# Handing a chunk's scaled rows from row layout to channel layout: VectorE squares and a trip through DRAM in place of TensorE transposes

## The chip, the core and the metric

The kernel runs on one core of a Trainium2 chip, in 32-bit floating point throughout. The core has five instruction queues: TensorE (PE; its weight loads are listed apart as PEld), VectorE (DVE), ScalarE (ACT), GpSimd (POOL) and SyncE (SP, which here only issues DMAs). Each queue runs its instructions in the order in which they were written, and an instruction that waits holds up everything behind it on its own queue; between queues the order is kept by semaphores. The metric is the device time in microseconds (us); lower is better. The kernel before takes 794.65 us, the median of 6 runs (792.32 to 797.26).

## The reference

Four sequences of 1024 tokens with 256 channels each go through an attention-like block (a gated linear recurrence along the sequence) and then a mixture of 8 experts of which each token takes 2; both halves are modulated per sequence. Cut to what matters:

```python
mod = (silu(c) @ wmod).reshape(4, 6, 1, -1)
sa, ca, ga, sb, cb, gb = (mod[:, i] for i in range(6))
ga, gb = clamped away from zero
h = layernorm(x) * (1 + ca) + sa
x = x + ga * attn(h)
h = layernorm(x) * (1 + cb) + sb
x = x + gb * ffn(h)

def attn(x):                                  # per sequence, D = 256, H = 512
    norm = l2norm(x) * D ** -0.5
    xn = rms_scale * x / (norm + EPS) * split_scale
    K = sigmoid(xn @ W_K)
    u, g_in, g_out = split(xn @ W_ugg, 3)
    u = u * sigmoid(g_in) * (1 - K)
    out = linear_scan(shifted K, u)           # s[t] = K[t-1] * s[t-1] + u[t]
    return out * sigmoid(g_out) @ W_out + x

def ffn(x):                                   # 8 experts, 256 -> 1024 -> 256
    scores = softmax(x @ Wg + bg); take the best 2, renormalise
    return sum over the 2 experts of score * (gelu(x @ W1[e] + b1[e]) @ W2[e] + b2[e])
```

## The kernel before

The 4096 tokens go through the first half in 8 chunks of 512 tokens (`for c_ in range(NCH)`, L990; two chunks make a sequence, `part` is 0 or 1). A chunk lies in two layouts: by rows (tokens on the 128 partitions, 4 groups of 128 tokens, 256 channels along the free axis) for the norms and the modulation, and by channels (`hT`: channels on the partitions, 2 groups of 128, 512 tokens along the free axis) as the moving operand of the projections. `ident` is the identity matrix that a TensorE transpose uses.

`project(c_, hc)` (L396) is called four times per chunk, once for each 128 of the 512 hidden channels. It makes four products of two matmuls each, `pk`, `pgi`, `pu`, `pgo`, in four PSUM banks that rotate (pool `ps_mm`, 4 buffers): so a product of one call can only start when the product of the same name of the call before has been read out of its bank. ScalarE reads `pk` (L421), `pgi` (L425) and `pgo` (L429), VectorE reads `pu` (L428), and then VectorE makes the recurrence (L431, L437, L438) into `z`. The list `mid` holds steps that are written between the reading of `pgi` and that of `pu`.

The order of all five queues is written out by hand (`manual_schedule`, L101). While chunk c is projected, three other pieces of work are threaded into the gaps:

- the head of chunk c+1, called `nxt`: the layer norm on ScalarE (`shift`, `a_norm`), modulation on VectorE (`a_mod`, L355 and L356), the sum of squares on ScalarE into tile `u` (`a_square`, L365), the root on VectorE and GpSimd (`a_root`, L371 and L372), the inverse and the scaling on VectorE (`a_scale`, L376, L377, L379), and the turning (`a_turn`, L387): 8 TensorE transposes of 128x128 into PSUM (L393) and two ScalarE evictions that also multiply each channel by `rs_sb` (L394). All of this happens within chunk c: `a_norm` in `project(c, 0)`, `a_square` in `project(c, 1)`, `a_scale` before `project(c, 2)`, `a_turn` in `project(c, 3)`.
- the tail of chunk c-1, called `prv`: the output projection (`o_pe`, L448, products `pya`), the residual (`o_resid`, L461, and its store L464), the second layer norm (`f_stats`, `f_norm`, `f_mod`, `f_store`), and `f_swap` (L503) at the chunk's end. `f_swap` already turns rows to channels without TensorE: VectorE transposes each 32x32 square of the rows into `u` (L508), SyncE stores that to DRAM (`swapped`, L512) and, once it has landed, loads it back with the squares exchanged in four loads (L519). The result `hT2` is the operand of the routing matmuls (`f_gate`, `pl`, L558) a chunk later.
- the routing of finished sequences, in some chunks only: `r_softmax`, `r_exp`, `r_first` in chunks 3, 5 and 7; `r_second` (some 18 small VectorE operations, L621 to L660), `r_rank_pe` (three small TensorE products `pr`, L667 to L674, on what `r_second` made) and `r_place` in chunks 4 and 6. `r_place` leaves 16 indirect scatters to the DRAM table `lists` (L580), which GpSimd issues six at a time in `drain` (L576).

Tile `u` has one buffer (`bufs=1`), shared by `a_square`/`a_scale` of the head and by `f_swap` of the tail: whoever writes it next waits until the one before has been read, and for `f_swap` the last reader is the DMA of L512.

In the last chunk SyncE starts the experts' weight loads (L837, L839) and the loads of the table entries (L808), GpSimd gathers the first block's rows (L820), and TensorE turns them in `project(7, 3)` (`b_turn(0)`, products `ptx`, L878). From 299 us on the second half runs: blocks of 256 rows of one expert, `b_up` (`ph`, L898) and `b_down` (`pye`, L928).

Of the kernel before, what the change touches and what calls it, by code (L numbers as in the profile page):

```python
# [19 lines left out]
def tile_adaln_block(  # L20
# [32 lines left out]
    nc = tc.nc  # L53
# [319 lines left out]

    def a_scale(c_):
        h, ss, u = X[c_]["h"], X[c_]["ss"], X[c_]["u"]
        nc.vector.tensor_scalar_add(ss, ss, RMS_EPS)  # L376
        nc.vector.reciprocal(ss, ss)  # L377
        for n in range(TPB):
            nc.vector.tensor_scalar_mul(u[:, n, :], h[:, n, :], ss[:, n : n + 1])  # L379

# [5 lines left out]

    def a_turn(c_):  # L387
        hT = deep.tile([P, KC, TB], F32, tag="hT", name=f"hT_{c_}")
        X[c_]["hT"] = hT
        for k in range(KC):  # L390
            pt = ps_tr.tile([P, TB], F32, tag="tr", name=f"pta_{c_}_{k}")
            for t in range(TPB):
                nc.tensor.transpose(pt[:, ts(t, P)], X[c_]["u"][:, t, ts(k, P)], ident)  # L393
            nc.scalar.activation(hT[:, k, :], pt, AF.Copy, scale=rs_sb[:, k : k + 1])  # L394

    def project(c_, hc, mid=()):  # L396


        hT = X[c_]["hT"]
# [8 lines left out]
        def product(w, col, what):  # L408
            ps = ps_mm.tile([P, TB], F32, tag="mm", name=f"p{what}_{c_}_{hc}")
            for k in range(KC):  # L410
                nc.tensor.matmul(  # L411
                    ps,
                    lhsT=w[:, k, col : col + P],
                    rhs=hT[:, k, :],
                    start=(k == 0),
                    stop=(k == KC - 1),
                )
            return ps
# [79 lines left out]


    turned = [P, NQ, KC, TPB, SQ]  # L500
    swapped = dram.tile([NQ, NQ, SQ, KC * TB // NQ], F32, tag="swapped", name="swapped")

    def f_swap(c_):  # L503


        u = work.tile([P, TPB, D], F32, tag="u", name=f"u2_{c_}", bufs=1)
        flat = u.rearrange("p n d -> p (n d)")
        nc.vector.transpose(  # L508
            flat.rearrange("p (q k n c) -> p n k q c", q=NQ, k=KC, n=TPB),
            X[c_]["h2"].rearrange("p n (k q c) -> p n k q c", k=KC, q=NQ),  # L510
        )
        nc.sync.dma_start(  # L512
            out=swapped.rearrange("q i c m -> (i c) q m"),
            in_=flat.rearrange("p (q m) -> p q m", q=NQ),
        )
        hT = deep.tile(turned, F32, tag="hT2", name=f"hT2_{c_}", bufs=1)
        X[c_]["hT2"] = hT
        for q in range(NQ):
            nc.sync.dma_start(  # L519
                out=hT[ts(q, SQ)].rearrange("p i k n t -> p i (k n t)"),  # L520
                in_=swapped[q].rearrange("i c m -> c i m"),
            )
# [456 lines left out]
    hT = deep.tile([P, KC, TB], F32, tag="hT", name="hT_0")  # L979
    X[0]["hT"] = hT  # L980
# [4 lines left out]
    nc.scalar.activation(hT[:, 0, :], pts[0], AF.Copy, scale=rs_sb[:, 0:1])  # L985
    nc.vector.tensor_scalar_mul(hT[:, 1, :], pts[1], rs_sb[:, 1:2])
# [3 lines left out]
    for c_ in range(NCH):  # L990
# [10 lines left out]
        if more:  # L1001
            shift(nxt)
        project(c_, 0, [lambda: a_norm(nxt)] if more else [])
        drain(6)
        if more:
            a_mod(nxt)
        if was:
            a_skip(c_)
            o_pe(prv)
            o_resid(prv)  # L1010
        if placed is not None:
            r_second(placed)
# [8 lines left out]
        project(c_, 1, [lambda: a_square(nxt)] if more else [])  # L1021
# [27 lines left out]
        if more:  # L1049
            a_root(nxt)  # L1050
# [6 lines left out]
        if more:  # L1057
            a_scale(nxt)
# [18 lines left out]
        project(c_, 3, [lambda: a_turn(nxt) if more else b_turn(0)])  # L1077
# [125 lines left out]
```

## Time and profile before

| | us |
|---|---|
| median of 6 runs | 794.65 (792.32 to 797.26) |
| the profiled execution's own time | 795.89 |
| its span, first to last instruction | 794.1 |
| chunk 4 (from the end of its first projection call to that of chunk 5) | 36.58 |
| chunk 5, the same | 36.02 |
| chunk 6, the same | 36.59 |
| TensorE busy in the span | 774.6 |

The profile is of one execution. Its instruction tables give a line of the kernel, the engine, the operation, the tiles (what is written, an arrow, what is read), how often, and how long. A timeline row gives start, duration and, in square brackets, how long the engine stood idle before it and what ended that. Matmuls overlap their neighbours, so the time that one costs TensorE is read from the distance between two starts, not from its duration: the four records of a 128x512 product show 1.88 us but start 1.72 us apart from the next product. A matmul in 32-bit floating point leaves two records; a transpose leaves one. "SPq" and "POOLq" are the queues that issue DMAs; a DMA row there is only the issue, and the landing is told apart.

### The profile page before, as it was taken

What the parts mean: (1) busy time and instruction counts of PE and PEld (TensorE: products, weight loads), DVE (VectorE), ACT (ScalarE), POOL (GpSimd) and SP (SyncE); (2) the same over time, 40 slices, a digit from 0 to 9 for tenths busy, and PEclk for the clock granted to TensorE, in tenths of its full rate; (3) what the DMA queues carried; (4) which work ended last, traced back from release to release, by engine and by line L of the source; (5) the groups of instructions that cost most, each with busy time, mean ns of one, the idle gap of its engine ahead of it and who ended that gap; (6) DMA issues with size and microseconds to landing.
All of it is one profiled execution on the core that took longest, in us unless ns stands there. A gap on an engine that the chain in (4) does not pass through costs nothing.

```text
span 794.1 us, 10818 instructions
## 1 busy us (share of the span) xinstructions
PE 774.6 (98%) x3279; PEld 579.1 (73%) x3279; DVE 506.7 (64%) x1369; ACT 241.8 (30%) x560; POOL 295.6 (37%) x372
## 2 busy tenths in 40 slices
PE   8999999999999999999999999999999999999974
PEld 5454545464555647888888888888888888888964
DVE  5787877899789968777453535454453535445653
ACT  4434243535354242322131222222131222213221
POOL 2102010107302830888843434343343424344421
PEclk9999999999999999999999999999999999999997
DMA  8221434052322367799797878777786787776691
GB/s 293 92 71 47 129 104 126 27 172 57 79 80 87 79 195 236 177 228 221 182 291 217 228 220 213 202 220 235 212 236 209 222 222 211 213 209 198 190 297 32
DMA packets 115463, 138.11 MB, mean 174 GB/s; under 512 B 25207, under 2 KB 99515, under 8 KB 115393
## 3 DMA queue, kind: packets, MB, share of 16 engines
q1 hardware_dynamic: 96368, 111.45, 47.2%
q0 software_dynamic: 17456, 25.25, 14.2%
q8 instruction: 32, 0.52, 0.3%
q10 hardware_dynamic: 1568, 0.57, 0.3%
q14 instruction: 39, 0.31, 0.1%
HBM read 114.31 MB, written 25.42 MB: 176 GB/s over the span
## 4 chain that ended last, share of the span: by engine, by line
PE 84%; DMA 7%; issue 3%; DVE 3%; ACT 1%; POOL 1%; POOLq 0%; SPq 0%; DVEq 0%
PE pye_False L928 24%; PE ph_False L898 24%; PE pya L448 7%; PE pk L411 7%; PE pgi L411 7%; PE pu L411 6%; PE pgo L411 6%; DMA out_dram<-yb_False,ent 3%; DMA hb<-hx,ent 3%; PE idle L257 1%; PE pta L393 1%; DMA ent<-lists 1%; PE pm L284 1%; DMA w<-in_L_ffn_W_dram 1%; POOL out_dram L915 1%
## 5 line engine op out<-in xcount | busy, mean ns | idle before, releaser
L928 PE MATMUL pye_False<-w,g_False 128*128 128x256 f32 x992 | 219.5, 379 | 0.0
L898 PE MATMUL ph_False<-xT,w 128*128 128x256 f32 x992 | 219.3, 379 | 0.0
L898 PEld LDWEIGHTS ph_False<-xT,w 128*128 128x128 f32 x992 | 188.3, 190 | 26.3 <-issue 0.5
L928 PEld LDWEIGHTS pye_False<-w,g_False 128*128 128x128 f32 x992 | 188.2, 190 | 25.9 <-issue 0.2
L907 ACT ACTIVATE g_False<-ph_False,bb 128x256 f32<-128x256 f32 x248 | 103.8, 470 | 301.4 <-issue 197.5
L885 DVE STREAM_TRANSPOSE xT<-hb 32x128 f32<-32x128 f32 x576 | 174.2, 302 | 21.5 <-DMA hb<-hx,ent 8.3
L942 DVE TENSOR_TENSOR yb_False<-pye_False,b2b 128x256 f32<-128x256 f32 x62 | 26.3, 424 | 185.7 <-PE pye_False L928 185.7
L915 POOL DMA_INDIRECT out_dram<-yb_False,ent x46 | 73.8, 1604 | 178.6 <-DVE yb_False L943 178.6
L580 POOL DMA_INDIRECT lists<-pay,placei x64 | 66.5, 1040 | 12.5 <-issue 11.0
L820 POOL DMA_INDIRECT hb<-hx,ent x56 | 58.9, 1051 | 20.7 <-issue 16.9
L411 PE MATMUL pk<-hT,wk_sb 128*128 128x512 f32 x128 | 61.0, 599 | 0.7 <-ACT hT L985 0.7
L411 PE MATMUL pu<-hT,wu_sb 128*128 128x512 f32 x128 | 60.2, 592 | 0.0
L411 PE MATMUL pgi<-hT,wu_sb 128*128 128x512 f32 x128 | 60.1, 592 | 0.0
L411 PE MATMUL pgo<-hT,wu_sb 128*128 128x512 f32 x128 | 60.1, 592 | 0.0
L448 PE MATMUL pya<-wo,z 128*128 128x256 f32 x256 | 56.6, 379 | 0.0
L217 POOL TENSOR_TENSOR rstd_f<-rstd_f,expo 128x4 f32<-128x4 f32 x8 | 8.1, 1018 | 128.9 <-DVE rstd_f L216 128.9
L448 PEld LDWEIGHTS pya<-wo,z 128*128 128x128 f32 x256 | 48.6, 190 | 9.5 <-issue 3.3
L411 PEld LDWEIGHTS pgi<-hT,wu_sb 128*128 128x128 f32 x128 | 24.3, 190 | 30.6 <-issue 30.4
L411 PEld LDWEIGHTS pgo<-hT,wu_sb 128*128 128x128 f32 x128 | 24.3, 190 | 30.6 <-issue 26.8
L421 ACT ACTIVATE kt<-pk 128x512 f32<-128x512 f32 x32 | 19.1, 598 | 82.5 <-PE pk L411 82.5
L411 PEld LDWEIGHTS pu<-hT,wu_sb 128*128 128x128 f32 x128 | 23.7, 190 | 26.8 <-issue 24.6
L411 PEld LDWEIGHTS pk<-hT,wk_sb 128*128 128x128 f32 x128 | 23.7, 190 | 26.0 <-issue 23.0
(195 smaller groups left out, 694.9 us busy)
## 6 DMA issues: line engine op xcount, KB each, us to landing
w<-in_L_ffn_W_dram SPq DMA_DIRECT2D x72, 1024.0 KB, 6.7
b2b<-in_L_ffn_b_dram SPq DMA_DIRECT2D x36, 128.0 KB, 6.4
hx<-gb SPq DMA_DIRECT2D x4, 1024.0 KB, 4.8
out_dram<-x SPq DMA_DIRECT2D x8, 512.0 KB, 3.3
hx<-h SPq DMA_DIRECT2D x8, 512.0 KB, 2.9
x<-in_L_attn_x_dram SPq DMA_DIRECT2D x7, 512.0 KB, 6.7
swapped<-u SPq DMA_DIRECT2D x7, 512.0 KB, 2.9
hT<-swapped SPq DMA_DIRECT2D x28, 128.0 KB, 2.8
```

What stands on the lines that cost most here:

```text
L217: nc.gpsimd.tensor_tensor(rstd, rstd, expo[:, 0, :], ALU.pow)
L411: nc.tensor.matmul(ps, lhsT=w[:, k, col : col + P], rhs=hT[:, k, :], start=(k == 0), stop=(k == KC - 1),)
L421: nc.scalar.activation(kt[:, 1:], ps, AF.Sigmoid)
L448: nc.tensor.matmul(py[:, t, :], lhsT=z[hc][:, ts(2 * q + t, P)], rhs=wo[:, hc, :], start=(hc == 0), stop=(hc == HC - 1),)
L580: ins = nc.gpsimd.indirect_dma_start(out=lists[:, :], out_offset=IndirectOffsetOnAxis(ap=place, axis=0), in_=what, in_offset=None, bounds_ ...
L820: nc.gpsimd.indirect_dma_start(out=hb[:, t, :], out_offset=None, in_=hx[: seen(j), :], in_offset=IndirectOffsetOnAxis(ap=BK[j]["ent"][:, t ...
L885: nc.vector.transpose(to[ts(q, SQ), :, :, ts(i, SQ)], hb[ts(i, SQ), :, :, ts(q, SQ)])
L898: nc.tensor.matmul(ph[:, u, :], lhsT=w1[:, k, ts(fc, P)], rhs=xT[:, k, :n], start=(k == 0), stop=(k == KC - 1),)
L907: nc.scalar.activation(g[:, fc, :n], ph[:, u, :], AF.Gelu_apprx_tanh, bias=bb[:, fc : fc + 1])
L915: return nc.gpsimd.indirect_dma_start(out=out_rows[:n], out_offset=IndirectOffsetOnAxis(ap=at, axis=0), in_=yb, in_offset=None, bounds_che ...
L928: nc.tensor.matmul(py, lhsT=g[:, fc, ts(t, P)], rhs=w2[:, fc, :], start=(fc == 0), stop=(fc == FC - 1),)
L942: nc.vector.tensor_add(yb, py, b2b)
```

## The change

For chunks 2 to 7 the head's rows are no longer turned by TensorE. Chunk 0 and chunk 1 keep their TensorE transposes (in a new output layout).

- Layout: `hT` of every chunk gets the layout that `hT2` had, `[P, NQ, KC, TPB, SQ]` (32-token runs), and `project` reads it through the view `by_channel`, so that its moving operand is 16 runs of 32 numbers, where it was 512 in a row.
- Scaling: `a_scale` on VectorE (4 operations) becomes `a_scale_squares` on ScalarE (4 activations), which write `u` square by square.
- Turning: `a_swap` turns `u` in place on VectorE (one operation over 128x1024) and sends it to DRAM and back with 1 + 4 DMAs on SyncE, in the way of `f_swap`, with a DRAM tile of its own. `a_channels` multiplies the result by `rs_sb` in place (two activations).
- Order: from chunk 2 on the head starts half a chunk sooner. `shift` and `a_norm` of chunk c+2 come in `project(c, 3)`, `a_mod` before `project(c+1, 0)`, `a_square` in `project(c+1, 0)`, `a_root` behind it, then `a_skip`, the inverse, `a_scale_squares`, `o_pe`, `o_resid`, `a_swap`, and `a_channels` in `project(c+1, 3)`.

```diff
+    def a_inverse(c_):
+        ss = X[c_]["ss"]
+        nc.vector.tensor_scalar_add(ss, ss, RMS_EPS)
+        nc.vector.reciprocal(ss, ss)
...
+    def a_scale_squares(c_):
+        h, ss, to = X[c_]["h"], X[c_]["ss"], by_square(X[c_]["u"])
+        for n in range(TPB):
+            nc.scalar.activation(
+                to[:, n], h[:, n, :].rearrange("p (k q c) -> p k q c", k=KC, q=NQ),
+                AF.Copy, scale=ss[:, n : n + 1],
+            )
...
+    def by_channel(hT):
+        return hT.rearrange("p i k n t -> p k n i t")
+
+    def swap(u, hT, by):
+        nc.sync.dma_start(
+            out=by.rearrange("q i c m -> (i c) q m"),
+            in_=u.rearrange("p n d -> p (n d)").rearrange("p (q m) -> p q m", q=NQ),
+        )
+        for q in range(NQ):
+            nc.sync.dma_start(
+                out=hT[ts(q, SQ)].rearrange("p i k n t -> p i (k n t)"),
+                in_=by[q].rearrange("i c m -> c i m"),
+            )
...
+    def a_swap(c_):
+        flat = X[c_]["u"].rearrange("p n d -> p (n d)")
+        nc.vector.transpose(flat, flat)
+        new_hT(c_)
+        swap(X[c_]["u"], X[c_]["hT"], swapped[0])
+
+    def a_channels(c_):
+        hT = by_channel(X[c_]["hT"])
+        for k in range(KC):
+            nc.scalar.activation(hT[:, k], hT[:, k], AF.Copy, scale=rs_sb[:, k : k + 1])
...
     def project(c_, hc, mid=()):
-        hT = X[c_]["hT"]
+        hT = by_channel(X[c_]["hT"])
...
-                    rhs=hT[:, k, :],
+                    rhs=hT[:, k],
...
-        if more:
+        if c_ == 0:
             shift(nxt)
-        project(c_, 0, [lambda: a_norm(nxt)] if more else [])
+        elif more:
+            a_mod(nxt)
+        project(c_, 0, [lambda: a_square(nxt) if was else a_norm(nxt)] if more else [])
         drain(6)
-        if more:
+        if c_ == 0:
             a_mod(nxt)
+        elif more:
+            a_root(nxt)
         if was:
             a_skip(c_)
+            if more:
+                a_inverse(nxt)
+                a_scale_squares(nxt)
             o_pe(prv)
             o_resid(prv)
+            if more:
+                a_swap(nxt)
...
-        project(c_, 1, [lambda: a_square(nxt)] if more else [])
+        project(c_, 1, [lambda: a_square(nxt)] if c_ == 0 else [])
...
-        if more:
+        if c_ == 0:
             a_root(nxt)
...
-        if more:
+        if c_ == 0:
             a_scale(nxt)
...
-        project(c_, 3, [lambda: a_turn(nxt) if more else b_turn(0)])
+        if nxt + 1 < NCH:
+            shift(nxt + 1)
+        project(
+            c_, 3,
+            [lambda: b_turn(0) if not more else a_channels(nxt) if was else a_turn(nxt)]
+            + ([lambda: a_norm(nxt + 1)] if nxt + 1 < NCH else []),
+        )
         drain(6)
         if was:
             f_swap(prv)
```

## The prediction

> **What bounds the kernel now.** I read four views: the page's engine shares and chain, the table of stretches, the timelines of the engines around one chunk, and SyncE's waits.
>
> ```profile
> PE 774.6 (98%) x3279; PEld 579.1 (73%) x3279; DVE 506.7 (64%) x1369; ACT 241.8 (30%) x560; POOL 295.6 (37%) x372
> ...
> PE 84%; DMA 7%; issue 3%; DVE 3%; ACT 1%; POOL 1%; POOLq 0%; SPq 0%; DVEq 0%
> ```
>
> TensorE is the chain. An operation taken off it is worth its own time, unless a wait takes its place. So: how much slack have the others?
>
> ```profile
> core 0: us, PE busy (x) PEld busy (x) DVE busy (x) ACT busy (x) POOL busy (x), PEclk, DMA share, GB/s
> 161.15:197.73 36.58, 36.58 (x127) 20.18 (x127) 34.77 (x84) 15.69 (x37) 15.86 (x27) 1.00 0.37 107
> 197.73:233.75 36.02, 36.02 (x122) 19.36 (x121) 29.41 (x64) 15.03 (x32) 9.69 (x12) 1.00 0.31 76
> 233.75:270.34 36.59, 36.59 (x128) 20.19 (x127) 34.66 (x89) 13.90 (x33) 15.85 (x26) 1.00 0.31 91
> ```
>
> These are chunks 4, 5 and 6, each from the end of its first projection call; columns: length, then busy time and instructions of each engine, TensorE's granted clock, the DMA share, GB/s. TensorE has no gap at a clock of 1.00. VectorE is busy 95% of chunks 4 and 6, where `r_second` and `r_place` run: there it is nearly a second bound.
>
> ```profile
> 186.40 1.04 PE L393 MATMUL pta<-ident,u 128*128 128x128 f32 x8
> 187.27 1.88 PE L411 MATMUL pu<-hT,wu_sb 128*128 128x512 f32 x4
> ```
>
> The TensorE timeline of chunk 4: eight transposes hold it from 186.40 to 187.27, 0.87 us.
>
> ```profile
> 195.88 0.36 SPq L512 DMA_DIRECT2D swapped<-u  x1
> 205.20 1.75 SPq L519 DMA_DIRECT2D hT<-swapped  x4
> ```
>
> ```profile
> SPq L519 <- DMA swapped<-u: 26.8, 7, 8.9
> ```
>
> SyncE's timeline at the end of chunk 4, and its waits. The store of `f_swap`'s `u` is issued at 195.88, and the loads that wait for it at 205.20: 9.3 us. The other chunks take 2.9 (for example issue at 158.70, loads at 161.66), chunk 6 5.6 (266.72 to 272.29). The two slow ones lie among GpSimd's scatters (L580, 181.87 to 204.23 and 254.47 to 276.89). Today nothing hurries: `a_square` writes `u` next at 208.60. Afterwards it comes half a chunk sooner.
>
> **The change part by part.** I laid each queue's new order end to end with the rows' durations. Distances between starts are duration less 0.08 us on VectorE and less 0.1 on ScalarE where nothing depends, plus 0.03 where it does.
>
> *Removed from TensorE*: 6 x 0.87 = 5.2 us (chunks 2 to 7; the order of instructions shows chunk 1's eight left). All on the path.
>
> *ScalarE*: two evictions go (L394, 686 ns each), two in-place activations of the same shape come in the same slot; their nearest row is L394, so 0. `a_norm` (L229, four in 2.06 us) moves ahead of the reading of `pgo`, where ScalarE idles 2.62 us: hidden, or about half a microsecond late for a bank that TensorE wants again three products (5.2 us) later. `a_scale_squares` adds four activations. No row has them: L365 (SBUF, 128x256, no scale pointer) takes 403 ns, L229 (two pointers) 588, and a pointer costs 686 - 598 = 88 ns (L394 against L421). I take 403 + 88 = 491, four in 1.66 us; ends 403 and 588. They stand ahead of the reading of `pk` in the second call.
>
> *VectorE*: `a_scale` goes (1.14 us), the square transpose comes; nearest is L508 (1239 ns, also 128x1024, to strided places, but not in place); ends 1.23 (L385, a plain operation of that size) and 2.5 (eight times L566's 0.31 for 128x128). The sum hardly moves, the place does: the inverse (0.38), the wait for ScalarE's last scaling (0.6) and the transpose (1.25) now come ahead of `r_second` and of the multiply that frees `pu`'s bank.
>
> *SyncE*: five more issues a chunk, 0.36 + 1.75 plus 2.95 of waiting, between the residual's store (170.27) and `f_store` (191.40). Queued behind are the `rows` loads, used over 10 us later: hidden. The loads land some 176 us in chunk 4's time, `a_channels` wants them at 185: 9 us of cover; past that every microsecond is TensorE's.
>
> *GpSimd*: no more work, but the root (L372, 1.01 us) now stands behind all 16 scatters of `drain`, which run 1.28 us apart. They end at about 204.4, 3.5 us before it is wanted; without the wait for `u` it would be wanted at once.
>
> *The new wait for `u`.* In chunk 5, `a_square` needs `u`, which `f_swap` of chunk 4 has just filled. Its store is issued at about 195.7. If it takes 9.3 us again, ScalarE waits to 205.0, and the reading of `pgo`, the root, the scalings and the reading of `pk` are queued behind. By rows: squares to 206.6, `pgo` read 207.2, `z` on VectorE 207.9, root on GpSimd 209.1 beside `a_skip` to 210.4, inverse 210.7, scalings 212.4, `pk` read 212.9. Only then is its bank free for the third call, which TensorE, then 3.1 us ahead, reaches at 209.8. Stall: 3.1 us.
>
> [...]
>
> *Chunks 4 and 6.* Before, VectorE makes `pr`'s operand `earlier` (L647) until 245.15, and TensorE takes it at about 247.4: 2.3 us of slack. Afterwards VectorE leaves chunk 5 some 3 us later (everything behind the stall), `r_first` ending at 236.3 instead of 233.3. From there: modulation to 238.8, recurrence and `z` to 242.2, `a_skip` to 244.7, inverse to 245.0, residual to 246.2, wait for the scalings to 246.7, transpose to 248.0, the nine operations of `r_second` up to `earlier` to 250.2. TensorE is there at 247.9: 2.3 us. Chunk 4 starts without that delay: 0.3. The first calls of chunks 5 and 6, whose `pu` multiply and `pgo` reading of the call before now stand behind the norm in `project(c, 3)`, cost 0.6 and 0.4.
>
> *The handover*: `ptx` waits for gathered rows. Before they land at 294.97 and TensorE is there at 295.03. The weight loads in front of the entries start when chunk 7's residual does, so they move with TensorE: 0.4 lost, 0.2 got back at `pr`. The second half then shifts as a whole.
>
> *A rule against it.* The Trainium skill ("VectorE: DVE Perf Modes", section "Rules for kernel authors") prefers TensorE for a full 128x128 turn where PSUM will do. The trace: 0.87 us on TensorE against 1.24 on VectorE and some 6 of DMA. By that rule alone the gain is at most 0; it doesn't weigh which engine is the bound.
>
> **Sum**: -5.2 + 3.1 (`u`) + 2.3 + 0.3 (`pr`) + 0.6 + 0.4 (first calls) + 0.4 - 0.2 (handover) = +1.7. On the profiled execution's 795.89 (794.1 of span, 1.8 around it) that is 797.6; this execution is 1.2 above the median of 794.65, so 796.4 is forecast.
>
> Ends, one at a time, laid out the same way: scaling 403 ns +0.6, 588 ns +2.9; transpose 2.5 us +5.4; `u`'s store 2.9 us -3.2, 7.5 us -0.1, 10.5 us (a little over the slowest) +2.9. Both cheap ends with a short store: -4.2. If a chunk's own store and loads were as slow as those among scatters (some 14 us), the 9 us of cover would be gone, and each such chunk would lose some 5.
>
> **Rivals.** A measurement tells changes from 0.3%, 2.4 us.
>
> *The store of `u` is short in chunk 5* (2.9 to 5.6). Its issue is 0.2 us from where it was, in the same scatters, which speaks against; the sister in chunk 6 took 5.6, which speaks for it. Then chunk 5's stall and most of chunk 6's lateness go: -2.0 to -4.2, middle -3.1, so 791.5.
>
> *TensorE reads the new `hT` more slowly*: the moving operand is 16 runs of 32 numbers. The place is all 512 records of L411, and no row has such a read. Near rows: 128x128 transposes come 0.87 / 8 = 0.109 us apart and a 128x512 record 1.72 / 4 = 0.43, so four short reads cost as much as a long one, which speaks for 0. For a price: L558's matmuls of 128 columns (0.57 us for 16 records) come 0.036 apart; if four run side by side, 128 columns take 0.143, a third more than a quarter of 0.43, and a third of 512 x 0.43 is 73 us, a far end. It decides from 5 ns a record (2.6 us): with that, 799.0 or more.
>
> *It doesn't do what it says*: TensorE's 0.87 us are filled by another wait in every chunk, near 0. In chunk 5 VectorE is idle 36.02 - 29.41 = 6.6 us, and the chunks without `r_place` are like it, which speaks against: 794.6.
>
> **How the numbers follow.** Forecast, `u` waits and chunk 6's `pr` is late: 0.55, its own range 794.2 to 800.1 (store 7.5 us; transpose 2.5); of it 0.30 lies within 0.3%, 0.25 above, since the dear ends outreach the cheap ones. Short store: 0.20 (0.17 faster, 0.03 within). Slower reads, or a dearer step that I gave 0: 0.20, slower. Nothing: 0.05. So faster 0.17, within 0.3% 0.38, slower 0.45. The range goes from the short store's middle, 791.5, to 800.5, a little past the dear end; what is left out is the tail of the slow reads and the cheapest end.
>
> **What would show it.** Right: no L393 after chunk 1; each of chunks 1 to 3 some 0.87 us shorter; in chunk 5 an idle TensorE before the third call's `pk`, released by ScalarE, with the first `u` square starting when the `swapped` store lands; in chunk 6 idle before `pr`, released by VectorE; the first gather's wait moved with chunk 7. Wrong: starts of L411 products other than 1.72 apart; a gap at the first product of a chunk (loads late); gaps in chunks 2 and 3; or no gap in chunk 5. If the store's time among scatters changes by 3 us, the sign changes.

## The result, and the profile after

The changed kernel takes 800.72 us (median of 20 runs, 798.71 to 804.92), the kernel before 794.36 in the same comparison: a ratio of 1.0086 (1.0073 to 1.0098), so slower by 0.9%, or 6.4 us, where +1.7 us was forecast. The profiled execution took 798.92 us, with a span of 797.2.

From the page of the changed kernel, the busy times and the shares of the chain that ended last:

```profile
PE 772.6 (97%) x3231; PEld 574.0 (72%) x3231; DVE 506.3 (64%) x1351; ACT 250.4 (31%) x584; POOL 299.9 (38%) x372
...
PE 70%; DVE 11%; DMA 10%; issue 4%; ACT 2%; POOL 2%; SPq 1%; POOLq 0%; DVEq 0%; ACTq 0%
```

TensorE is busy 2.0 us less than before (774.6), though 5.2 us of transposes are gone: about half of the missing 3.2 us is a lower clock, told below, which made other products 1.7 us longer. The second line says more. Before, the chain was TensorE for 84% and VectorE for 3%. Now 11% of it is VectorE and 10% DMA: some stretch is no longer TensorE's.

The table of stretches for chunks 4 to 7 (length; busy time and instructions of TensorE, its weight loads, VectorE, ScalarE, GpSimd; granted clock, DMA share, GB/s):

```profile
158.12:195.47 37.35, 36.69 (x120) 19.19 (x119) 34.20 (x82) 15.19 (x37) 14.80 (x23) 1.00 0.48 132
195.47:234.77 39.30, 35.99 (x113) 18.22 (x113) 28.46 (x54) 17.79 (x38) 11.95 (x16) 1.00 0.36 91
234.77:274.49 39.72, 37.90 (x120) 19.93 (x119) 36.89 (x95) 13.71 (x33) 15.48 (x24) 0.96 0.41 123
274.49:313.19 38.70, 37.05 (x139) 22.47 (x139) 27.94 (x60) 15.28 (x26) 14.74 (x18) 1.00 0.61 161
```

Chunks 1 to 3 became 0.89, 0.86 and 0.89 us shorter, as forecast (34.37, 35.15 and 35.14 us). Chunks 4 to 7 became longer by 0.77, 3.28, 3.13 and 1.12. With 0.39 us won before chunk 1 this adds up to 5.27, which is how much later the second block's first product `ph` starts (324.07 before, 329.33 now, a rounding apart). From there on the distance stays: the last of the whole blocks comes at 697.17 in place of 691.90. What follows the second `ph` takes 466 to 472 us in the traces of this study (but for one comparison, told below), in no order with the change, so the experiments are read at the second `ph`. About 1 us of the 6.4 between the medians isn't seen there and is not followed up.

The stalls, from TensorE's timeline (start, duration, in brackets the idle time before and what ended it):

```profile
211.20 0.65 PE L600 MATMUL pl<-hT,wg_sb 128*32 128x128 f32 x16 [1.88 <-DMA hT<-swapped]
213.10 1.98 PE L471 MATMUL pk<-hT,wk_sb 128*128 128x512 f32 x4 [1.25 <-ACT kt L481]
...
249.93 0.43 PE L709 MATMUL pr<-chose,before 128*128 128x64 f32 x2 [1.38 <-DVE chose L676]
250.81 0.43 PE L712 MATMUL pr<-earlier,ones 128*128 128x64 f32 x2 [0.44 <-DVE earlier L689]
...
251.92 3.14 PE L471 MATMUL pk<-hT,wk_sb 128*128 128x512 f32 x4
254.86 2.46 PE L471 MATMUL pgi<-hT,wu_sb 128*128 128x512 f32 x4
257.16 1.88 PE L471 MATMUL pu<-hT,wu_sb 128*128 128x512 f32 x4
```

In chunk 5 TensorE waits for `hT2` before `pl` and then for the bank of `pk`; in chunk 6 for VectorE's `chose` and `earlier` before `pr`. The two lines after that were not expected: `pk` and `pgi` behind `pr` take 2.94 and 2.30 us to the next start, where 1.82 and 1.72 were usual in this place: 1.7 us more. `pu` to `pgo` is 1.72 again. The products that read the new layout therefore cost nothing extra: the rival of the slower reads falls with this view.

SyncE's timeline for the store of `u` at the end of chunk 4, and its waits (us in total, times, the longest):

```profile
195.45 0.36 SPq L419 DMA_DIRECT2D swapped<-u  x1
205.07 1.75 SPq L424 DMA_DIRECT2D hT<-swapped  x4
```

```profile
SPq L424 <- DMA swapped<-u: 44.4, 13, 9.2
```

The store is issued at 195.45 and its loads at 205.07: 9.6 us, as slow as before the change (9.3), and now something waits for it. There are 13 such waits where there were 7, the longest 9.2. Last, from the chain that ended last between 150 and 305 us, the pieces that matter here (start, length, what):

```profile
167.36 1.71 ACT u L394 x4
169.10 1.25 DVE u L435
...
195.45 9.54 DMA swapped<-u
...
212.60 1.25 DVE u L435
...
247.24 1.25 DVE u L435
...
250.81 0.43 PE pr L712 x2
...
252.00 3.07 PE pk L471 x4
...
274.49 6.92 PE pya L508 x32
...
297.33 3.53 DMA hb<-hx,ente
```

ScalarE's scalings (L394) and VectorE's square transpose (L435) lie on the chain, and so does the store; then come `pr`, the slow `pk`, `pya` of chunk 7 and the gather of the first block's rows (`hb`).

### The profile page after: what moved, and what is told of

The parts are those of the page before. It is cut to its first block, busy times and chain, and to the rows that moved or that the text cites. A ratio compares the mean times of both kernels' runs of the same rounds, so it can differ in the third digit from the quotient of the medians.

```text
span 797.2 us, 10775 instructions
## 1 busy us (share of the span) xinstructions
PE 772.6 (97%) x3231; PEld 574.0 (72%) x3231; DVE 506.3 (64%) x1351; ACT 250.4 (31%) x584; POOL 299.9 (38%) x372
## 4 chain that ended last, share of the span: by engine, by line
PE 70%; DVE 11%; DMA 10%; issue 4%; ACT 2%; POOL 2%; SPq 1%; POOLq 0%; DVEq 0%; ACTq 0%
PE pye_False L970 23%; PE ph_False L940 23%; PE pya L508 4%; PE pk L471 4%; PE pgi L471 4%; PE pu L471 4%; DMA out_dram<-yb_False,ent 4%; PE pgo L471 4%; DMA hb<-hx,ent 2%; DVE s L497 1%; DMA swapped<-u 1%; DVE z L498 1%; DMA out_dram<-last_y,last_at 1%; PE idle L257 1%; POOL lists L622 1%
## 5 line engine op out<-in xcount | busy, mean ns | idle before, releaser
L372 POOL TENSOR_TENSOR ss<-ss,expo 128x4 f32<-128x4 f32 x8 | 13.1, 1641 | 79.2 <-DVE ss L371 79.2
L217 POOL TENSOR_TENSOR rstd_a<-rstd_a,expo 128x4 f32<-128x4 f32 x8 | 12.6, 1574 | 68.2 <-DVE rstd_a L216 68.2
```

Of the source, the lines that this page charges most:

```text
L217: nc.gpsimd.tensor_tensor(rstd, rstd, expo[:, 0, :], ALU.pow)
L372: nc.gpsimd.tensor_tensor(ss, ss, expo[:, 1, :], ALU.pow)
```

## The experiments

Two theories stood at the beginning. A: the stalls seen on TensorE are the loss, and taking away what makes each gives back its length. B: the lower clock in chunk 6 was an accident of that execution. In the short diffs below "-" is the changed kernel.

**The same kernel again.**

> The changed kernel a second time, for a second trace of the same program. Theory A (the extra loss follows from the queues): in chunk 5 TensorE waits again some 3.5 us in all at the routing matmul and the next pk, in chunk 6 some 2.2 us around pr, and in chunk 6 the granted clock falls again (1.8 us more for pk and pgi, 3.07 and 2.26 us in place of 1.72 each); second ph some 5.3 us later than before the change. Theory B (the clock drop was an accident of one execution): the waits are there again, the clock stays at 1.00 and the second ph is only some 3.5 us later. Ratio to before 1.006 to 1.010 in either case.

Ratio 1.0081 (1.0058 to 1.0104), second `ph` at 328.33. TensorE's timeline and the table of stretches:

```profile
210.30 0.64 PE L600 MATMUL pl<-hT,wg_sb 128*32 128x128 f32 x16 [1.50 <-DMA hT<-swapped]
212.38 3.68 PE L471 MATMUL pk<-hT,wk_sb 128*128 128x512 f32 x4 [1.43 <-ACT kt L481]
```

```profile
208.00:212.50 4.50, 1.56 (x19) 0.53 (x18) 3.77 (x7) 2.36 (x6) 1.40 (x1) 1.00 0.18 53
212.50:215.90 3.40, 3.40 (x5) 1.32 (x6) 3.33 (x12) 0.79 (x2) 0.93 (x1) 0.50 0.83 279
```

The clock fell again, to 0.50 for 3.4 us, but in chunk 5. In chunk 6 it did not. Yet the second `ph` is only 1.0 us earlier: what chunk 6 lost less, the wait for gathered rows (`ptx`, 1.54 and 1.13 us) took. Two stalls of different size with nearly the same end: a first sign against adding stalls up.

**Squares into another buffer.** ScalarE's throw-away squares go into the coming `hT`, so that they don't wait for `u`; only the scaling takes `u` (`new_u` is the allocation that stood in `a_square`).

```diff
     def a_square(c_):
-        u = work.tile([P, TPB, D], F32, tag="u", name=f"u_{c_}", bufs=1)
-        X[c_]["u"] = u
+        if c_ == 0:
+            spare = X[c_]["u"] = new_u(c_)
+        else:
+            new_hT(c_)
+            spare = X[c_]["hT"].rearrange("p i k n t -> p (i k n t)")
+            spare = spare.rearrange("p (n d) -> p n d", n=TPB)
...
-                u[:, n, :], h[:, n, :], AF.Square, accum_out=ss[:, n : n + 1]
+                spare[:, n, :], h[:, n, :], AF.Square, accum_out=ss[:, n : n + 1]
...
     def a_scale_squares(c_):
+        X[c_]["u"] = new_u(c_)
```

> The throw-away squares of a_square go into the buffer of the coming hT, which is free at that time, so ScalarE no longer waits for the store of f_swap's u before the squares; only the scalings need u. If the wait for u is the term that sets chunk 5 (theory A): the squares start at some 198.5 instead of 205.1, the scalings at the landing of the store (205), the bank of pk is read at 207 and TensorE does not wait for it; the wait of the routing matmul for hT2 (1.9 to 2.1 us) stays, since the store still takes 9 us. VectorE leaves chunk 5 some 2 us earlier, so the stall at pr in chunk 6 goes from 2.2 to about 0.5 and the clock drop behind it (1.8) goes too. Time some 4 to 5 us under the changed kernel, ratio to before 1.002 to 1.004. If the clock drop has another cause: only 3 us under it, 1.005. If the loss is in reading the new layout or in something spread over all chunks: no change, 1.008 or more.

Ratio 1.0051 (1.0033 to 1.0068). The squares start at 198.11, the wait for `pk`'s bank is gone, the wait of `pl` is 2.45 us. The scalings start at 206.36, not 205: the root stands behind the scatters on GpSimd. `pr` waits 0.45 us. By theory A that should have given 4 to 5 us; against the changed kernel in the same comparison it gave 1.6 (798.18 beside 799.8), and 0.5 at the second `ph` (327.82). Part of the shortfall is again the clock, which fell behind the wait of `pl` (`pk` took 3.12 us), so this run alone doesn't refute theory A.

**`r_second` ahead of the swap.**

```diff
-            if more:
-                a_swap(nxt)
         if placed is not None:
             r_second(placed)
+        if was and more:
+            a_swap(nxt)
```

> In chunks 4 and 6 r_second stands ahead of a_swap on VectorE. Theory A: the operand of pr is ready 1.9 us earlier (0.66 us of waiting for ScalarE's scalings and 1.25 us of transpose no longer stand ahead), the stall at pr in chunk 6 falls from 2.2 us to about 0.3 and in chunk 4 from 0.8 to nothing; if the clock drop comes from the idle stretch, its 1.8 us go with it: 4 to 4.5 us under the changed kernel, ratio to before 1.003. Chunk 5's 3.5 us stay. Theory B (the clock drop is independent of that idle stretch): 2.5 us under it, 1.005. Against both: the swap moves 3.4 us closer to the scatters; if its store and loads come among them (9 us and 5 us), a_channels in chunks 4 and 6 is late and as much is lost again, ratio 1.007 or more.

Ratio 1.0068 (1.0042 to 1.0094). The stall at `pr` shrank as expected (0.23 us in chunk 6, none in chunk 4), and the clock stayed up there. But the second `ph` comes at 328.28: `ptx` now waits 2.68 and 1.26 us, and the clock falls behind that. Stalls that are taken away come back at `ptx`.

**Scatters held back.** The 16 scatters of chunk 4 start after chunk 5's root.

```diff
         project(c_, 0, [...])
-        drain(6)
+        if c_ != 5:
+            drain(6)
...
             a_root(nxt)
+        if c_ == 5:
+            drain(6)
...
-        drain(6)
+        if c_ != 4:
+            drain(6)
```

The last hunk stands behind both `project(c_, 2)` and `project(c_, 3)`.

> GpSimd's scatters of the batch placed in chunk 4 are held back until after the root in chunk 5 (the drains behind the third and fourth projection call of chunk 4 are left out there, and the one in chunk 5 comes after a_root), so none is in flight when f_swap's store of chunk 4 is issued. Theory A (the scatters make that store slow, and the slow store makes chunk 5's stall, chunk 6's lateness at pr and the clock drop): the store takes 3 us instead of 9.6, the waits of the routing matmul and of pk in chunk 5 vanish (3.5 us), the pr stall in chunk 6 falls to about 0.5, no clock drop: 6 to 7 us under the changed kernel, ratio to before 0.999 to 1.001. The scatters now run from some 205 to 225 beside a_swap's store in chunk 5, which may take 9 us; it has 9 us of cover, and what is over costs 1 to 3 us. Theory B (the store is slow for a reason of its own place, such as what SyncE issues before it): it stays near 9 us, and the time stays at 1.008.

Ratio 1.0027 (1.0007 to 1.0047). SyncE's timeline:

```profile
194.27 0.36 SPq L419 DMA_DIRECT2D swapped<-u  x1
197.28 1.75 SPq L424 DMA_DIRECT2D hT<-swapped  x4
...
206.08 0.38 SPq L419 DMA_DIRECT2D swapped<-u  x1
214.48 1.75 SPq L424 DMA_DIRECT2D hT<-swapped  x4
```

`f_swap`'s store now takes 3.0 us (194.27 to 197.28), and `a_swap`'s, which now lies among the scatters (202.53 to 223.42), takes 8.4. So the scatters make a store slow, whichever of the two lies among them. Chunk 5's waits are gone altogether. But `pr` in chunk 6 still waited 1.40 and 0.44 us, where 0.5 was expected, and 3.8 us of the lead over the kernel before were lost between chunk 7's `pya` (268.16 beside 270.18) and the second `ph` (325.81 beside 324.07).

**A third theory.** All four say that the second half starts when the first block's rows are there, whatever TensorE does in chunks 5 to 7. So I followed those rows backwards. VectorE's timeline, before and after: from `f_swap` at the end of chunk 5 to `r_place` in chunk 6.

```profile
230.04 1.24 DVE L508 STREAM_TRANSPOSE u<-h 128x1024 f32<-128x1024 f32 x1
...
253.49 0.22 DVE L687 TENSOR_TENSOR key<-pick,rank 128x64 f32<-128x64 f32 x1
```

```profile
233.50 1.24 DVE L560 STREAM_TRANSPOSE u<-h 128x1024 f32<-128x1024 f32 x1
...
247.24 1.25 DVE L435 STREAM_TRANSPOSE u<-u 128x1024 f32<-128x1024 f32 x1 [0.66 <-ACT u L394]
...
259.03 0.22 DVE L729 TENSOR_TENSOR key<-pick,rank 128x64 f32<-128x64 f32 x1
```

The only idle time that VectorE's timeline lists in this stretch is the 0.66 us in brackets. It took 23.45 us and takes 25.53: transpose 1.17 (to the next start), wait 0.66, the inverse's two operations 0.29. GpSimd's timeline, the first and the last of the 16 scatters and the second gather, before and after:

```profile
254.47 1.04 POOL L580 DMA_INDIRECT lists<-pay,placei  x1 [0.33 <-DVE key L687]
...
275.92 0.97 POOL L580 DMA_INDIRECT lists<-pay,placei  x1 [0.19 <-issue]
...
291.38 1.06 POOL L820 DMA_INDIRECT hb<-hx,ente  x1 [0.31 <-issue]
```

```profile
260.00 1.03 POOL L622 DMA_INDIRECT lists<-pay,placei  x1 [4.24 <-DVE key L729]
...
281.13 0.97 POOL L622 DMA_INDIRECT lists<-pay,placei  x1 [0.19 <-issue]
...
297.33 1.01 POOL L862 DMA_INDIRECT hb<-hx,ente  x1 [0.31 <-issue]
```

And TensorE's, where it takes these rows:

```profile
295.03 0.60 PE L878 MATMUL ptx<-ident,hb 128*128 128x128 f32 x4
```

```profile
299.49 0.30 PE L920 MATMUL ptx<-ident,hb 128*128 128x128 f32 x1 [0.16 <-DMA hb<-hx,ente]
300.91 0.55 PE L920 MATMUL ptx<-ident,hb 128*128 128x128 f32 x3 [1.11 <-DMA hb<-hx,ente]
```

The first scatter comes 5.5 us later (260.00 beside 254.47), the second gather 5.95, and `ptx` runs on the second gather at 300.91 in place of 295.03. In every trace of this study the loads of the table entries begin 5.8 to 7.0 us after the last scatter, and `ptx` takes the second gather's rows 40.3 to 41.2 us after the first scatter (in one kernel, the last below, TensorE itself comes later than that). Ways of nearly the same length lead there. One goes by `r_place`, the scatters and their landing: SyncE waited for that in six of the experiments, 1.1 to 2.2 us, and there the loads begin 5.8 to 6.5 us after the last scatter. Before the change they began 6.3 us after it, so this way had about half a microsecond of slack at most. The other goes by `pr`, TensorE, chunk 7's residual and the weight loads ahead of the entries (as in the chain above). Both leave from VectorE's routing work in chunk 6. Before the change `ptx` started the moment its rows were there.

Theory H of the expectations, then: from chunk 4 on VectorE's queue sets the start of the second half. The times at which it passes five marks, and what lies between:

| | `f_swap`, end of chunk 3 | `r_place`, chunk 4 | `f_swap`, end of 4 | `f_swap`, end of 5 | `r_place`, chunk 6 |
|---|---|---|---|---|---|
| before | 157.43 | 180.88 (+23.45) | 194.61 (+13.73) | 230.04 (+35.43) | 253.49 (+23.45) |
| after | 155.36 | 180.89 (+25.53) | 194.19 (+13.30) | 233.50 (+39.31) | 259.03 (+25.53) |
| order alone (second run) | 157.38 | 181.03 (+23.65) | 194.35 (+13.32) | 231.12 (+36.77) | 254.78 (+23.66) |
| TensorE's turn in 4 and 6 (second run) | 155.06 | 178.71 (+23.65) | 192.02 (+13.31) | 231.09 (+39.07) | 254.76 (+23.67) |
| three together (second run) | 154.94 | 178.60 (+23.66) | 190.80 (+12.20) | 226.68 (+35.88) | 250.33 (+23.65) |

VectorE enters chunk 4 2.07 us ahead, loses 2.08 in it, is 0.43 faster to the end of chunk 4, loses 3.88 in chunk 5 (the wait for the slow store) and 2.08 in chunk 6: 5.54 late. At `r_place` of chunk 4 TensorE's whole gain was already used up on VectorE. The two other traces of the changed kernel agree: their first scatter comes 4.8 and 5.4 us late, in the first 5.5.

**A cost for VectorE alone, in the kernel before.** Nothing of the change; two more of `scale_out`'s multiplies (L346, the same values to the same place) just ahead of `r_place` in chunk 6.

```diff
+        if c_ == 6:
+            for _ in range(2):
+                nc.vector.tensor_mul(WO[b], wo_sb, MDF[b][:, 0, :].unsqueeze(1).broadcast_to((P, HC, D)))
         if placed is not None:
             r_place(placed)
```

> The kernel before the change, with scale_out's multiply of chunk 6 done two more times on VectorE (same values to the same place, 1.22 us each) just ahead of r_place. Nothing is added for TensorE. Theory H: from f_swap of chunk 5 to the first scatter VectorE's queue has no idle time that hides it, so the first scatter comes 2.3 to 2.5 us later (254.5 to 256.9) and the second ph with it (324.1 to 326.4): ratio 1.003. Rival (VectorE has slack there, TensorE alone sets the time): the scatters move by less than 1 us and the second ph by nothing, ratio 1.000.

Ratio 1.0040 (1.0019 to 1.0061). The first scatter on GpSimd, and TensorE at `ptx`:

```profile
256.77 1.04 POOL L580 DMA_INDIRECT lists<-pay,placei  x1 [1.81 <-DVE key L687]
```

```profile
296.20 0.30 PE L878 MATMUL ptx<-ident,hb 128*128 128x128 f32 x1 [1.11 <-DMA hb<-hx,ente]
297.50 0.88 PE L878 MATMUL ptx<-ident,hb 128*128 128x128 f32 x3 [1.01 <-DMA hb<-hx,ente]
```

2.3 us more at the scatter (254.47 before), and TensorE, which has the same work as before and until here the same times (`pya` of chunk 7 at 270.08), waits 1.11 and 1.01 us for rows. Behind that wait the clock falls (0.58 over 298.0 to 301.5), and the second `ph` is 3.5 us late (327.61): 2.3, and 1.2 behind the lower clock. VectorE, "64% busy" on the page, has no slack here. By which way the delay went is another matter; from the chain that ended last:

```profile
278.33 1.20 DVE x L461 x2
...
288.76 3.27 DMA ente<-lists
```

It stays on VectorE up to chunk 7's residual (L461), whose store and the weight loads stand ahead of the entries on SyncE; SyncE doesn't wait for the scatters to land. So the run shows that VectorE's queue sets the start of the second half, not that the scatters carry the delay.

**TensorE's turn kept in chunks 4 and 6.** The swap stays for the rows of chunks 2, 3, 4 and 6.

```diff
+    def a_scale_plain(c_):
+        h, ss, u = X[c_]["h"], X[c_]["ss"], X[c_]["u"]
+        for n in range(TPB):
+            nc.scalar.activation(u[:, n, :], h[:, n, :], AF.Copy, scale=ss[:, n : n + 1])
...
-                a_scale_squares(nxt)
+                (a_scale_squares if placed is None else a_scale_plain)(nxt)
...
-            if more:
+            if more and placed is None:
                 a_swap(nxt)
...
-            [... a_channels(nxt) if was else a_turn(nxt)]
+            [... a_channels(nxt) if was and placed is None else a_turn(nxt)]
```

> In chunks 4 and 6, in which VectorE also runs r_second and r_place, the next chunk's rows are turned by TensorE again (0.87 us each, scaled by ScalarE into plain rows); the swap stays for chunks 2, 3, 4 and 6's rows only. Theory H (VectorE's queue in chunk 6 sets the first scatter, and the second half starts 40.5 us after the first scatter, whatever TensorE does): from f_swap of chunk 5 to the first scatter VectorE needs 26.5 us in the changed kernel (233.50 to 260.00) and 24.4 before; without transpose, wait and inverse's place it needs 24.5 again, so the first scatter comes at some 258 and the second ph at some 327.3, 2 us earlier than in the changed kernel, though TensorE has 1.7 us more to do. Ratio to before 1.005 to 1.006. Theory P (TensorE's own stalls add up): pr stalls in chunks 4 and 6 go from 0.8 and 2.2 to some 0.2, less 1.7: 1 us earlier, ratio 1.007. The 3.5 us in chunk 5 stay under both.

The second `ph` came at 325.63, first scatter at 256.12, better than expected, and the ratio was 0.9947 (0.9919 to 0.9975). But in this comparison the kernel before took 809.21 us (802.88 to 814.83), and in all four of its traces the second half had waits that no other trace shows (TensorE busy 342.5 to 348.4 of the 355 us from 345 to 700, elsewhere 355.0). The ratio contradicts the trace, so it was measured again beside the changed kernel:

> TensorE's turn in chunks 4 and 6 a second time. If the start of the second half sets the time (theory H): second ph some 1.5 us later than before, 797 to 798 beside 795 or ratio 1.001 to 1.003, and some 3 us under the changed kernel. If the first ratio, 0.9947, holds: 3 to 5 us faster than before, and the handover does not explain the time.

Ratio 1.0005 (0.9990 to 1.0019), second `ph` at 325.09. The first ratio was that comparison's disturbance; the second lies between theory H's 1.001 and no change. VectorE needs 23.67 us again where it needed 25.53. The second `ph` comes 4.2 us sooner than in the first trace of the changed kernel, where theory H had forecast 2: it had left out chunk 4, whose share (192.02 beside 194.19 at its end) came through chunk 5 as well.

**The order alone.** No square transpose and no swap: `a_scale_plain` as above in every chunk, `a_swap` left out, `a_turn(nxt)` in place of `a_channels(nxt)`, and the head half a chunk sooner as in the change.

> The earlier order alone: norm, modulation, squares, root and scaling half a chunk sooner as in the change, but all chunks turned by TensorE as before the change (no square transpose, no swap; ScalarE scales into plain rows). Theory O (the order costs by itself, through u's wait in chunk 5 and the norm in the last calls): chunk 5 stalls 3.5 us at pk, the first calls of chunks 5 and 6 lose 0.8 and 0.7, nothing is saved, so the second ph comes some 5 us later than before and the ratio is 1.006 to 1.008. Rival S (the loss is in the swap itself: VectorE's transpose, the DMAs, the strided reading): the order alone is near no change, 1.000 to 1.002.

And the second time:

> The order alone a second time. Theory H: second ph some 1.4 us later than before, ratio 1.001 to 1.003. If the first ratio, 0.9988, holds: no change to 1 us faster.

0.9988 (0.9954 to 1.0021) in the disturbed comparison, 1.0001 (0.9982 to 1.0020) in the other, second `ph` at 325.46 and 325.30. Theory O's 5 us are wrong: with 0.87 us more in each chunk TensorE reaches the third call's `pk` later, and the stall there is only 0.65 us. The order is nearly free (the second `ph` 1.4 and 1.2 us later, the time in the second comparison unchanged within 0.2%); taking the transposes off TensorE on top of it made the kernel 0.8% slower. The third run of the changed kernel, in the same comparison:

> The changed kernel beside the two: second ph 4.2 to 5.3 us later than before, ratio 1.006 to 1.009; one clock drop somewhere in chunks 5 to 7.

Ratio 1.0082 (1.0061 to 1.0103), second `ph` at 330.25, with two clock drops, in chunk 5 and behind `ptx`.

**Idle stretches filled.** Throw-away transposes of the identity in TensorE's queue (`pad` is a bank of `pta`'s pool).

```diff
+        if c_ == 6:
+            fill(10, "pr")
         if placed is not None:
             r_rank_pe(placed)
+        if c_ == 5:
+            fill(14, "pl")
         if been:
             f_gate(old)
+        if c_ == 5:
+            fill(8, "pk")
```

> The changed kernel with throw-away 128x128 transposes put into TensorE's idle stretches: 14 before the routing matmul of chunk 5, 8 behind it, 10 before pr of chunk 6. Theory C (the granted clock falls after a stretch of some 4 us in which TensorE is idle for more than half): with these stretches filled it stays at 1.00 in chunks 5 and 6, and no pk or pgi takes more than 1.9 us. Rival: the clock falls there all the same (it follows something else). On time: if the drop counts in full, 1.8 us under the changed kernel (ratio 1.006); by theory H (the second half starts 40.5 us after the first scatter, set by VectorE in chunk 6) only the part that VectorE waits for, 0 to 0.9 us (1.007 to 1.008).

The table of stretches (the granted clock stands ahead of the last two columns):

```profile
209.00:213.00 4.00, 3.79 (x41) 2.86 (x39) 3.27 (x7) 2.30 (x6) 0.96 (x1) 1.00 0.15 43
248.00:252.00 4.00, 3.22 (x34) 2.43 (x33) 3.66 (x19) 0.68 (x2) 0.00 (x0) 1.00 0.63 211
...
301.00:304.50 3.50, 3.50 (x7) 1.63 (x6) 0.69 (x1) 0.00 (x0) 2.01 (x2) 0.52 0.93 304
```

Where the stretches are filled the clock stays at 1.00. It falls behind the one that was left, the wait at `ptx` (0.52 in the last line). The second `ph` comes at 330.87, no earlier than in the traces without filling (328.33 to 330.25): in this trace the drop only moved to a place where nothing hides it. The ratio, 1.0108 (1.0074 to 1.0142), is from the disturbed comparison and says little. As the clock fell at different places in the three traces of the changed kernel, one trace in which it held where TensorE was kept busy supports theory C but doesn't prove it.

**`scale_out` behind `r_place`**, in chunks 4 and 6 of the changed kernel.

> The changed kernel with scale_out's multiply (L346, 1.22 us) of chunks 4 and 6 moved behind r_place. Theory H: in chunk 6 the time from f_swap of chunk 5 to the last place falls from 25.5 to 24.4 us, the first scatter and the second ph come 1.1 us sooner in chunk 6 and, by chunk 4, up to 1.1 more: 1 to 2 us under the changed kernel. By TensorE's own sum nothing changes.

VectorE's stretches in chunks 4 and 6 fell to 24.39 us, as expected. But in chunk 4 the multiply only moved behind `r_place`: VectorE ends the chunk at 194.49 (194.19 without the move), so nothing of that share is left. In chunk 5 the clock was low for some 6 us (`pk` and `pgi` took 3.57 and 2.93 us). First scatter 259.43, second `ph` 328.12, 1.2 us sooner than in the first trace of the changed kernel, ratio 1.0063 (1.0042 to 1.0084). The interval overlaps that of the unchanged order.

**Three together, and a fourth.** Squares aside, TensorE's turn in chunks 4 and 6, and the scatters held back (6 behind chunk 5's root, 6 behind its second call, 4 behind its fourth); then the same with `scale_out` behind `r_place`.

> Three of the suspected costs taken away together: squares into the coming hT's buffer, TensorE's turn in chunks 4 and 6, and the scatters of chunk 4's batch held back (6 after chunk 5's root, 6 after its second call, 4 after its fourth). By theory H: chunks 1 to 3 keep their 2.6 us, chunk 5 its 0.9, nothing stalls in chunks 4 to 6 but the norm in the last calls (0.3 to 0.8 each); pya of chunk 6 starts at some 230.5 in place of 233.6, the first scatter comes at 251 to 252 in place of 254.5, and the second ph at some 321 to 322 in place of 324.1: 2 to 3 us faster than before, ratio 0.996 to 0.9975. If something else holds the handover (a clock drop behind the wait for gathered rows, the chain from scatters to rows longer than 40.5 us): 1.000 or more.

The three a second time, and with the fourth:

> The three together a second time, beside the version with scale_out moved and beside the kernel before: second ph at some 321, first scatter at 251.6, ratio 0.994 to 0.997, as in the first run on another chip. If that first ratio (0.9948) came from that chip, on which the kernel before took 809 us: ratio 1.000.

> The three together (squares aside, TensorE's turn in chunks 4 and 6, scatters held back) and scale_out of chunks 4 and 6 behind r_place. By theory H the first scatter comes at 250.4 in place of 251.6 and the gathered rows land 1.2 us sooner, at 291.3; TensorE reaches ptx at 291.1 then, so second ph some 1 us sooner, at 320, 4 us sooner than before the change: ratio 0.993 to 0.996. If TensorE's own work is the bound there by now: no change against the version without it, second ph at 320.9.

Three together: 0.9948 (0.9917 to 0.9979) in the disturbed comparison, 0.9963 (0.9949 to 0.9977) in the other, 790.29 beside 793.27 us, second `ph` at 320.92 and 320.71. With `scale_out` moved: 0.9955 (0.9941 to 0.9969), 789.38 us, second `ph` at 319.94, and no wait at `ptx` at all. Both beat both kernels. (The record has the same chip number for both comparisons, so the first ratio can't be put down to another chip.) The page of the three together, second run:

```profile
PE 769.1 (98%) x3247; PEld 573.1 (73%) x3247; DVE 504.1 (64%) x1349; ACT 250.7 (32%) x584; POOL 301.0 (38%) x372
...
PE 82%; DMA 10%; issue 3%; DVE 2%; POOL 1%; POOLq 0%; SPq 0%; ACT 0%; DVEq 0%
```

TensorE is the chain again (82%), VectorE 2% of it. Four turns of 0.87 us, 3.5 us in all, are off TensorE, and the second `ph` comes 3.2 and 3.4 us sooner.

## Why the prediction was wrong, point by point

- *The 0.87 us a chunk*: right in chunks 1 to 3. What failed is counting all six as "on the path". From chunk 4 on TensorE's own time isn't what sets the start of the second half.
- *The wait for `u`*: right in mechanism and place. Store 9.6 us (9.3 assumed), ScalarE's squares at 205.10, `pk` read at 212.47; stall 3.4 us, 3.1 forecast. A second wait stood ahead of it, `pl` for `hT2`, whose loads follow the same store. It cost nothing by itself here, since `pk` would have waited to 213.0 in any case; with the squares aside it was what remained.
- *`pr` in chunks 4 and 6*: 0.8 and 2.3 us where 0.3 and 2.3 were forecast. *First calls of chunks 5 and 6*: 0.8 and 0.7 where 0.6 and 0.4 were.
- *Prices*: four scalings 1.70 us (1.66), transpose 1.25 (1.25), reading `hT` 0: all good.
- *The handover, "they move with TensorE: 0.4 lost, 0.2 got back"*: the step that failed. I had seen that the rows land at 294.97 and TensorE is there at 295.03, and took the zero slack for a small wait. It was the junction of a second path without slack, and that path leaves from VectorE, which I had called "nearly a second bound". I priced VectorE's later `r_second` only as an idle TensorE at `pr`, and did not ask when `r_place` and its scatters come. TensorE's own sum (+1.5 us without the handover) was not far off: chunk 7's `pya` starts 4.1, 1.7 and 2.3 us late in the three traces, of which some 1.5 to 1.7 each are the clock. But the second `ph` is 5.3, 4.3 and 6.2 us late, so from there on 1.1, 2.5 and 3.9 us are lost where 0.2 was forecast (the last with the second clock drop, 1.7). By the table of marks the sum is -2.07 + 2.08 - 0.43 + 3.88 + 2.08 = +5.54, and 5.27 of it is seen at the second `ph`.
- *The clock*, a term that the sum puts at nothing without a word: each of the three traces of the changed kernel shows the drop, 1.4 to 1.7 us of longer products a time, the third shows two. In the first it lies on the chain; in the second most of it was hidden, since TensorE would have waited at `ptx` anyway.
- *Rivals*: the short store did not happen, and its price was wrong too: with the scatters held back the store took 3.0 us, and the kernel was still slower than before (1.0027, 1.0007 to 1.0047), not 3 us faster. So the sign did not hang on the store alone, as the prediction's last sentence has it. The slow reads are excluded by the starts 1.72 us apart, and "does nothing" by chunks 1 to 3.

The Trainium skill ("DMA: Bandwidth & Descriptors", section "Anatomy of one DMA — SWDGE (gpsimd) path") gives a fixed 2 us plus bytes over 436 GB/s for DMAs that GpSimd issues. Carried over to this store of SyncE's it would be an estimate of 3.2 us. Away from the scatters the store took 2.9 to 3.8 us here; among them it took up to 9.6.

What stays open: why the clock falls behind one of two nearly equal idle stretches and not the other, and how a scatter slows a store of another queue. That TensorE reaches the gathered rows first in the last version, so that the next bound is its own work again, is read from one trace.

## What to carry to other kernels

An engine that is 64% busy over the span can still set the time if its work is full in the two chunks from which a later stage is released: look for every point where two paths meet without slack, and price a moved operation on each of them, not only as a stall of the busiest engine. If an operation is taken off the bound by giving it to a second engine, do it only in the stages in which that second engine has room: here four swaps out of six, with the order and buffers mended, gave 0.4%, and all six cost 0.9%. A stall that is removed ahead of such a junction comes back at it.

## What the runs showed of the hardware

- A 512 KB store by SyncE took 2.9 to 3.8 us away from GpSimd's indirect scatters (128 rows each, 1.28 us apart). It took 7.4 to 9.6 us where six or seven scatters were issued in its time, whichever of the two stores that was, and 4.7 to 5.9 us where one to five were. One store issued 5.6 us behind the last scatter took 4.8 us.
- After idle stretches of TensorE of 2 to 4 us in all, the granted clock fell to 0.50 for some 3 to 4 us, a loss of 1.4 to 1.7 us (in one trace for some 6 us, 3.0 us lost). Nine of the traces of chunks 5 to 7 show it, at different places in identical programs; not every such stretch does (1.11 and 1.01 us at `ptx` were followed by a drop in one kernel, 1.15 and 1.12 were not in another), and in the one trace with filled stretches none that had been filled. The Trainium skill ("TensorE: Matmul & The Clock Gate", section "Part 1: The HAM clock gate (the "warmup" mystery)") describes a free-running window of about 3.4 us and half the clock after an idle one. The length and the half agree with the rows; but ahead of the drop in the second trace TensorE was busy for 1.56 of 4.5 us and no idle piece was longer than 1.50 us, so there was no wholly idle window.
